# The output matrix of an attention layer: from seven block products (two by two by two) to fifteen (two by three by three)

## The chip, the cores and the metric

The kernel runs on one core of a Trainium2 chip. The metric is the device time of one execution in microseconds; the times shown are medians of several runs. The engines of a core are TensorE (PE in the profile, with PEld for its weight loads), VectorE (DVE), ScalarE (ACT), GpSimd (POOL) and SyncE (SP), which in this kernel issues all DMAs.

## The reference

Two graph layers act on `x` of 128 graphs x 64 nodes x 768 features, that is 8192 rows of 768, with an adjacency matrix for each graph. All arithmetic is float32.

```python
# layer 0: a graph attention with 12 heads of 64, a gate, residual, layer norm
x = _layernorm(x + _L0_gnn_ref(x, adj, W, b, w_src, w_dst, H_w, H_b))
# layer 1: masked attention with 6 heads of 128, residual, layer norm
q = heads(x @ Wq + bq); k = heads(x @ Wk + bk); v = heads(x @ Wv + bv)
scores = einsum('bhqd,bhkd->bhqk', q, k) / sqrt(128)
probs = softmax(scores + where(adj, 0, -9e15))
ctx = einsum('bhqk,bhkd->bhqd', probs, v)          # back to rows of 768
x = _layernorm(x + ctx @ Wf + bf)
```

The change concerns the last line alone: the product of the context (8192 x 768) with `Wf` (768 x 768), the bias and the rows `x` that are added, and the norm.

## The kernel before

Rows are worked in tiles of 128 (two graphs); four tiles make a quad, and there are 16 quads. Phase A computes layer 0 for all tiles, stores its rows (`x1_there`), and computes layer 1's values (`v_there`). Phase B, the second half of the time, does the rest of layer 1, a quad at a time, in three rounds `f` = 0, 1, 2 of two heads each: queries (7 products), keys (7 products), then the "slab" `slab(Q, f)`: scores, masked softmax, transposes by DMA, context.

All large matrix products are made by a scheme with fewer multiplications than the plain one. Both operands are cut in two by two blocks; sums of blocks are formed on each side, and 7 products of blocks instead of 8 give the result (the Winograd form of Strassen's scheme). `TURNS` lists the seven: name, PSUM tile (of three), block of the tokens, block of the weights. A product's reader is called when it is done; some results are sums of several products, gathered in PSUM (a product adds onto what its tile holds) or by DVE.

For the output (`output`, line 1026) a group is two tiles `ya`, `yb` of one quad: their context's four blocks are 128 tokens x 384 features, `Wf`'s are 384 x 384. A product is three matmuls of 128 x 128 stationary tokens against 384 columns of weights. Each quad has two groups, so there are 32 of 7 products. `operands` (line 1003) forms the four sums of context blocks on DVE; `rows_of` (line 1013) loads the rows of the first layer from DRAM by SP and adds the bias on POOL (line 1023); in the group ACT copies the first product (1042), DVE makes six adds from PSUM (1047 to 1066), and POOL three adds of rows (1036). `normed` (1071) takes mean and variance on DVE, the power on POOL (335), scales on ACT (1077) and stores by SP (1079).

The order of work is written by a host-side clock, `Beat`: each product is one beat; work is queued "so many beats from now", a reader 1.5 beats after its product was issued. A generator started with `beat.start` is taken up again after as many beats as it yields. Every engine runs its instructions in the order in which they were so issued, and semaphores are put where one engine needs another. So times in beats set orders, not durations.

In quad `q` the round loop (1088 to 1108) issues queries, then (rounds 1 and 2) starts the previous quad's `operands` and `rows_of`, then keys, then the slab, then the previous quad's output group: group 0 in round 1, group 1 in round 2. Products have 5 PSUM tiles in phase B, taken in turn as they come free. The matrix `Wf` is loaded at the start of phase B into the place of `Wv` (12 DMAs of `matrix`, line 243), its four block sums made by POOL, and `last_bias` adds `bv @ Wf` to the bias.

Of the kernel before, what the change touches and what calls it, by code (L numbers as in the profile page):

```python
# [31 lines left out]
ALU = mybir.AluOpType  # L35
# [4 lines left out]
P = 128  # L40
N = 64
D = 768
KC = D // P
KH = KC // 2
HALF = D // 2
H0, E0 = 12, 64
H1, E1 = 6, 128
BANK = 512
# [8 lines left out]
W11, W21, W22, T1, T2, T3, N4 = range(7)  # L57
# [13 lines left out]
    ("P4", 1, X22, N4),  # L71
)

# [50 lines left out]
class Beat:  # L127
# [23 lines left out]
        time = self.now + after + 0.7  # L151
        self.at(time, lambda: step(time), order)

    def product(self, emit, then):
        emit()
        self.at(self.now + 1.5, then)
        self.tick()

    def tick(self):
        while self.events and self.events[0][0] < self.now + 1:  # L160
            heapq.heappop(self.events)[-1]()
        self.now += 1

    def until(self, there):
        while not there():
# [8 lines left out]
def two_layers(  # L174
# [21 lines left out]
    nc = tc.nc  # L196
    n_tiles = x.shape[0] // P
    n_quads = n_tiles // 4
    n_pairs = n_tiles // 2
    beat = Beat()  # L200
# [5 lines left out]
    def sb(pool, shape, tag, name, bufs=None, dtype=F32):  # L206
        return pool.tile(shape, dtype, tag=tag, name=name, bufs=bufs)
# [8 lines left out]
    bv_sb = const.tile([P, KC], F32, name="bv_sb")  # L216
# [3 lines left out]

    places = [const.tile([P, 7, KH, HALF], F32, name=f"w_{i}") for i in range(3)]
    place = {"w0": 0, "h_w": 1, "wv": 2, "wq": 0, "wk": 1, "wf": 2}
# [20 lines left out]
    def matrix(w, name, engine, gap):  # L243

        t = places[place[name]]
        blocks = w.rearrange("(k c p) (m n) -> k m p c n", k=2, p=P, m=2)
        for at, k, m in ((W11, 0, 0), (T3, 0, 1), (W22, 1, 1), (W21, 1, 0)):
            for c in range(KH):
                nc.sync.dma_start(t[:, at, c], blocks[k, m][:, c])
                yield gap  # L250
        yield 3
        for to, a, b in ((T1, T3, W11), (T2, W22, T1), (T3, W22, T3), (N4, W21, T2)):
            for c in range(KH):
                engine.tensor_tensor(t[:, to, c], t[:, a, c], t[:, b, c], ALU.subtract)
                yield gap
        ready[f"{name}_sb"] = t
# [30 lines left out]
    def sums_of_tokens(engine, s, b11, b12, b21, b22):  # L287

        if engine is nc.vector:
            plus(s[:, 0], b21, b22)  # L290
            plus(s[:, 1], s[:, 0], b11, ALU.subtract)
            yield 1
            plus(s[:, 2], b11, b21, ALU.subtract)
            plus(s[:, 3], b12, s[:, 1], ALU.subtract)
        else:
            engine.tensor_tensor(s[:, 0], b21, b22, ALU.add)
            engine.tensor_tensor(s[:, 1], s[:, 0], b11, ALU.subtract)
            yield 1
            engine.tensor_tensor(s[:, 2], b11, b21, ALU.subtract)
            engine.tensor_tensor(s[:, 3], b12, s[:, 1], ALU.subtract)  # L300
# [47 lines left out]
    def in_zone(at, *shape):  # L348
        size = math.prod(shape)
        letters = " ".join("abc"[: len(shape)])  # L350
        sizes = dict(zip("abc", shape))
        return zone[:, at : at + size].rearrange(f"p ({letters}) -> p {letters}", **sizes)
# [507 lines left out]
    blocks = {}  # L860
# [9 lines left out]


    def phase_b(pb, ps_b):
        beat.start(matrix(wf, "wf", nc.gpsimd, 1), 2)
        bf_sb = row(bf, "bf_sb", pb)

        def last_bias():

            for m, parts in enumerate((((0, W11), (1, W21)), ((0, W11), (0, T1), (1, W22)))):
                ps = sb(dense[0], [P, BANK], "dense", f"bias_ps_{m}")[:, 0:HALF]
                steps = [(k * KH + c, wb, c) for k, wb in parts for c in range(KH)]  # L880
                for i, (at, wb, c) in enumerate(steps):
                    nc.tensor.matmul(  # L882
                        ps,
                        lhsT=bv_sb[:, at : at + 1].to_broadcast([P, P]),
                        rhs=ready["wf_sb"][:, wb, c, :],
                        start=(i == 0),
                        stop=(i == len(steps) - 1),
                    )
                to = bf_sb[:, m * HALF : (m + 1) * HALF]
                nc.vector.tensor_tensor(to, to, ps, ALU.add)  # L890

        def part(name):
            return sb(pb, [P, HALF], "part", name, 7)

        def load(Q):

# [106 lines left out]
        def operands(Q, i):  # L1003

            while not Q.get("done"):
                yield 1
            q, c = Q["q"], Q["c"][i]
            s = sb(pb, [P, 4, KH, P], "sc", f"sc_{q}_{i}", 1)
            b = [c[:, 0, :, 0], c[:, 1, :, 0], c[:, 0, :, 1], c[:, 1, :, 1]]
            yield from sums_of_tokens(nc.vector, s, *b)  # L1010
            Q["ob", i] = b + [s[:, k] for k in range(4)]

        def rows_of(Q, i):
            q = Q["q"]
            for k in range(2):
                t = 4 * q + 2 * k + i
                y = sb(pb, [P, D], "y", f"y_{t}", 4)
                nc.sync.dma_start(y, x1_there[t])
                Q["y", i, k] = y
            yield 2  # L1020
            for k in range(2):
                y = Q["y", i, k]
                nc.gpsimd.tensor_tensor(y, y, bf_sb, ALU.add)  # L1023
                yield 1

        def output(Q, i):
            q = Q["q"]
            ya, yb = Q["y", i, 0], Q["y", i, 1]
            lo, hi = slice(0, HALF), slice(HALF, D)
            u = {}  # L1030
            name = f"o_{q}_{i}_"

            def with_rows(k, of, y, m):
                def work():
                    u[k] = part(f"{name}{k}")
                    nc.gpsimd.tensor_tensor(u[k], u[of], y[:, m], ALU.add)  # L1036

                beat.soon(work)

            def p1(ps):  # L1040
                u[1] = part(f"{name}1")
                nc.scalar.copy(u[1], ps)
                with_rows(4, 1, yb, lo)

            def p6(ps):
                u[2] = part(f"{name}2")
                nc.vector.tensor_tensor(u[2], u[1], ps, ALU.add)
                with_rows(5, 2, ya, hi)

            def p2(ps):  # L1050
                nc.vector.tensor_tensor(ya[:, lo], ya[:, lo], ps, ALU.add)

            def p5(ps):
                u[3] = part(f"{name}3")
                nc.vector.tensor_tensor(u[3], u[1], ps, ALU.add)
                with_rows(6, 3, yb, hi)

            def p7(ps):
                nc.vector.tensor_tensor(yb[:, hi], u[6], ps, ALU.add)

            def p4(ps):
                nc.vector.tensor_tensor(yb[:, lo], u[4], ps, ALU.add)
                beat.start(normed(yb, 4 * q + 2 + i), 0)

            def p3(ps):
                nc.vector.tensor_tensor(ya[:, hi], u[5], ps, ALU.add)
                beat.start(normed(ya, 4 * q + i), 0)

            by_token(name, Q["ob", i], ready["wf_sb"], dict(P1=p1, P2=p2, P3=p3, P4=p4, P5=p5, P6=p6, P7=p7))

        def normed(y, t):
            scale = variance_to_scale(y, EPS, f"1_{t}")
            rs = next(scale)
            yield 1
            next(scale, None)
            yield 1
            nc.scalar.activation(y, y, AF.Identity, bias=rs[:, 1:2], scale=rs[:, 0:1])
            yield 1
            nc.sync.dma_start(out[t * P : (t + 1) * P, :], y)

        Q, before = quads[0], None

        def at_place(q, f):

            return (None, 0, 1)[f]

        load(Q)
        for q in range(n_quads + 1):
            for f in range(3):
                if q < n_quads and (q or f):  # L1090
                    queries(q, f, blocks, part)
                if q == 1 and f == 0:
                    last_bias()
                if before and at_place(q, f) is not None:
                    i = at_place(q, f)
                    beat.start(operands(before, i))
                    beat.start(rows_of(before, i))
                if q < n_quads:
                    then = None
                    if f == 2 and q + 1 < n_quads:  # L1100
                        then = lambda xb: blocks.update({xb: load_block(q + 1, xb)})
                    if q or f:
                        keys(q, f, blocks, part, then)
                    beat.start(slab(Q, f), 1)
                if before and at_place(q, f) is not None:
                    beat.until(lambda: ("ob", i) in before)
                    output(before, i)
            before, Q = Q, quads.get(q + 1)
# [57 lines left out]
```

## Time and profile before

| what | us |
|---|---|
| median of 3 runs | 2870.66 (2870.18 to 2870.84) |
| the profiled execution's own time | 2870.47 |
| its span, first to last instruction | 2868.7 |
| PE busy | 2819.2 |
| DVE busy | 1864.5 |
| ACT busy | 1324.9 |
| POOL busy | 1149.5 |

The profile is of one execution. Its parts used below: busy time per engine; the chain of work that ended last; groups of instructions by line, with operation, tiles, shapes, count, then busy time and mean duration, then the idle time of the engine before them and what ended it; and the timeline, which gives start, length, engine, line, operation and count. Durations of pipelined instructions overlap, so distances between starts are used for PE. An fp32 matmul shows as two MATMUL records.

### The profile page before, as it was taken

To read this page: it belongs to the slowest core of one execution; us is meant where nothing else is said; L and a number is where in the kernel's file an instruction comes from. 1 tells how busy PE (TensorE), PEld (TensorE's weight loads), DVE (VectorE), ACT (ScalarE), POOL (GpSimd) and SP (SyncE) were. 2 spreads that over 40 slices of the span, in tenths; PEclk is the share of its full clock that TensorE was granted. 3 is DMA by queue.
4 is the path that set the end of the run, shared out by engine and by line. 5 is a ranking of instruction groups with operands and counts; after the bars stand their busy time and mean duration, and the time that the engine had idled before them with its cause. 6 is when DMAs were issued, how large, how long until landed. Compare 5 with 4: busy or idle time off the path is not lost.

```text
span 2868.7 us, 42091 instructions
## 1 busy us (share of the span) xinstructions
PE 2819.2 (98%) x15586; PEld 1924.7 (67%) x15586; DVE 1864.5 (65%) x3567; ACT 1324.9 (46%) x1594; POOL 1149.5 (40%) x1022
## 2 busy tenths in 40 slices
PE   7899999999999999999899999999999999999998
PEld 4455555555555555555577878778787787877775
DVE  6888888888888888888634444444444444444444
ACT  2655665665665665655433333334333333333332
POOL 6656666665665665665412121221111211112113
PEclk9999999999999999999999999999999999999999
DMA  6666766666666766766655345534455443454432
GB/s 205 161 166 169 179 165 170 182 163 171 181 164 169 186 160 167 188 164 193 194 132 124 92 113 131 120 98 103 102 131 124 99 108 96 128 124 108 110 94 77
DMA packets 626285, 409.50 MB, mean 143 GB/s; under 512 B 440224, under 2 KB 572320, under 8 KB 626080
## 3 DMA queue, kind: packets, MB, share of 16 engines
q1 hardware_dynamic: 626080, 406.81, 55.0%
q8 instruction: 123, 2.02, 0.3%
q14 instruction: 82, 0.67, 0.1%
HBM read 186.69 MB, written 119.93 MB: 107 GB/s over the span
## 4 chain that ended last, share of the span: by engine, by line
PE 94%; DVE 2%; DMA 1%; ACT 0%; issue 0%; POOL 0%; SPq 0%; POOLq 0%; DVEq 0%; ACTq 0%
PE o L311 15%; PE k L407 15%; PE q L407 15%; PE v L311 15%; PE g L311 14%; PE h L311 14%; PE f_all L707 2%; PE s_ps L920 2%; PE c_ps L976 2%; DMA th_d<-bc_e 0%; PE bias_ps L882 0%; DVE th_d L651 0%; ACT bc_e L698 0%; DMA elu_turned<-xg_parts 0%; DVE st L328 0%
## 5 line engine op out<-in xcount | busy, mean ns | idle before, releaser
L311 PE MATMUL h<-w,zone 128*128 128x384 f32 x1320 | 445.8, 494 | 21.0 <-ACT h L498 12.2
L407 PE MATMUL q<-zone,w 128*128 128x256 f32 x2016 | 450.1, 381 | 3.5 <-issue 1.2
L407 PE MATMUL k<-zone,w 128*128 128x256 f32 x2016 | 446.2, 381 | 0.9 <-ACT k_u L387 0.9
L311 PE MATMUL g<-w,zone 128*128 128x384 f32 x1320 | 441.3, 489 | 4.6 <-DVE gate L552 3.8
L407 PEld LDWEIGHTS q<-zone,w 128*128 128x128 f32 x2016 | 381.3, 190 | 64.7 <-issue 3.4
L407 PEld LDWEIGHTS k<-zone,w 128*128 128x128 f32 x2016 | 380.6, 190 | 57.0 <-issue 5.0
L1023 POOL TENSOR_TENSOR y<-y,bf_sb 128x768 f32<-128x768 f32 x64 | 114.8, 1815 | 704.1 <-DMA y<-x_there 640.6
L311 PEld LDWEIGHTS h<-w,zone 128*128 128x128 f32 x1320 | 250.3, 192 | 193.4 <-ACT h L498 13.4
L311 PEld LDWEIGHTS g<-w,zone 128*128 128x128 f32 x1320 | 247.5, 190 | 176.6 <-DVE gate L552 13.3
L311 PE MATMUL o<-w,sc 128*128 128x384 f32 x768 | 268.0, 493 | 2.8 <-DVE sc L280 2.8
L311 PE MATMUL v<-w,x_sums 128*128 128x384 f32 x768 | 258.5, 486 | 1.8 <-DVE x_sums L280 1.8
L335 POOL TENSOR_TENSOR rs<-rs,power 128x1 f32<-128x1 f32 x128 | 71.2, 556 | 459.3 <-DVE rs L333 459.3
L627 POOL TENSOR_TENSOR bc_e<-th_d,w_dst_sb 128x768 f32<-128x768 f32 x64 | 119.9, 1874 | 290.4 <-ACT th_d L522 253.0
L311 PEld LDWEIGHTS v<-w,x_sums 128*128 128x128 f32 x768 | 145.7, 190 | 104.1 <-DVE x_sums L280 3.1
L311 PEld LDWEIGHTS o<-w,sc 128*128 128x128 f32 x768 | 144.1, 191 | 99.9 <-DVE sc L280 3.8
L311 PE MATMUL o<-w,cT 128*128 128x384 f32 x576 | 203.3, 489 | 0.5 <-ACT cT L986 0.5
L1036 POOL TENSOR_TENSOR o<-o,y 128x384 f32<-128x384 f32 x96 | 107.4, 1119 | 182.0 <-issue 82.0
L990 ACT COPY parts<-c_ps 128x1024 uint16<-128x1024 uint16 x94 | 95.4, 1015 | 149.8 <-PE c_ps L976 149.8
L311 PEld LDWEIGHTS o<-w,cT 128*128 128x128 f32 x576 | 108.0, 190 | 72.5 <-issue 2.6
L622 POOL TENSOR_SCALAR zone<-zone 128x768 f32<-128x768 f32 x64 | 137.2, 2144 | 0.0
L615 ACT ACTIVATE gate<-gate 128x768 f32<-128x768 f32 x64 | 53.9, 843 | 167.4 <-DVE gate L558 118.5
L698 ACT COPY bc_e<-th_d 128x1536 uint16<-128x1536 uint16 x64 | 123.3, 1927 | 14.6 <-DMA th_d<-bc_e 14.6
(161 smaller groups left out, 4492.6 us busy)
## 6 DMA issues: line engine op xcount, KB each, us to landing
zone<-ops_there SPq DMA_DIRECT2D x224, 192.0 KB, 4.7
zone<-in_xT SPq DMA_DIRECT2D x32, 768.0 KB, 6.6
zone<-in_x SPq DMA_DIRECT2D x64, 384.0 KB, 3.8
bc_e<-there SPq DMA_DIRECT2D x128, 192.0 KB, 3.5
x_there<-mix SPq DMA_DIRECT2D x64, 384.0 KB, 4.2
ops_there<-x_sums SPq DMA_DIRECT2D x32, 768.0 KB, 3.3
v_there<-v SPq DMA_DIRECT2D x128, 192.0 KB, 2.6
v<-v_there SPq DMA_DIRECT2D x128, 192.0 KB, 3.8
```

Source lines behind the costliest of these rows:

```text
L311: nc.tensor.matmul(ps, lhsT=blocks[xb][:, c, :], rhs=w[:, wb, c, :], start=(c == 0 and to not in begun), stop=(c == KH - 1), skip_group_ch ...
L335: nc.gpsimd.tensor_tensor(rs[:, 0:1], rs[:, 0:1], power, ALU.pow)
L407: nc.tensor.matmul(ps, lhsT=w[:, wb, c, f * P : (f + 1) * P], rhs=blocks[xb][:, c, :], start=(c == 0 and to not in begun), stop=(c == KH - 1),
L622: nc.gpsimd.tensor_scalar(xs, xs, 1.0, None, ALU.add)
L627: nc.gpsimd.tensor_tensor(bc, th, w_dst_sb, ALU.mult)
L698: nc.scalar.copy(halves(e), by_halves(d))
L707: nc.tensor.matmul(f_all[b * N : (b + 1) * N, at : at + E0 + 1], lhsT=e[rows, hd // 2 * P + b * N : hd // 2 * P + (b + 1) * N], rhs=(h[row ...
L920: nc.tensor.matmul(s_ps[b * N : (b + 1) * N, i, r, :], lhsT=qT[:, r, at], rhs=kT[:, r, at], start=True, stop=True,)
L976: nc.tensor.matmul(c_ps[cols, r, i, :], lhsT=sT[rows, i, cols], rhs=v_of, start=True, stop=True)
L990: nc.scalar.copy(by_halves(parts), halves(c_ps[:, r].rearrange("p i t -> p (i t)")))
L1023: nc.gpsimd.tensor_tensor(y, y, bf_sb, ALU.add)
L1036: nc.gpsimd.tensor_tensor(u[k], u[of], y[:, m], ALU.add)
```

## The change

The output's product is cut otherwise: the group's two tiles of tokens by three parts of the inner dimension by three parts of the columns. A context block is now 128 tokens x 256 features, a weight block 256 x 256, and the plain way would need 18 block products; a scheme with 15 is used. A product is two matmuls against 256 columns.

- `FIFTEEN` lists the products: PSUM tile (of six), block or sum of the context, block of the weights, and the places (of six: two tiles by three thirds) onto which the PSUM tile is added or from which it is subtracted. A PSUM tile gathers up to five products and is read after each of them.
- The reads go straight into the rows `y` on DVE, in place: 16 per group. The ACT copy, the six DVE adds and the three POOL adds are gone.
- `operands` makes eleven sums of 256 features x 128 tokens instead of four of 384, one per yield, and is started before the queries of its round rather than after. For the very last group most of these are made on POOL, in the zone that held the query operands.
- `rows_of` is started earlier: group 0's rows in round 2 of its own quad, group 1's in round 0 of the next, and it waits (in host order) until the bias is ready and the previous quad's rows of the same group have been sent out. The ring of row buffers still has four.
- `Wf` comes in nine DMAs of 256 KB, its blocks' sums are 15 POOL operations of 512 columns, and the bias is made in three parts between the first quad's queries.
- `Beat.product` and `tick` take a length; an output product counts 2/3 of a beat. The pool of parts has 5 buffers of 256 columns instead of 7 of 384.

```diff
+FIFTEEN = (
+    (0, "3", 9, ((-1, 1),)),
+    (2, "A2", 6, ((1, 0),)),
+    (1, "12", 0, ((-1, 3),)),
+    (0, "11", 7, ((1, 4),)),
...
+    (0, "1", 8, ((1, 0), (-1, 2))),
+    (5, "6", 13, ((-1, 4),)),
+    (1, "0", 10, ((1, 5),)),
+)
...
-    def product(self, emit, then):
+    def product(self, emit, then, length=1):
         emit()
-        self.at(self.now + 1.5, then)
-        self.tick()
+        self.at(self.now + 1.5 * length, then)
+        self.tick(length)
...
-        beat.start(matrix(wf, "wf", nc.gpsimd, 1), 2)
...
+        def last_matrix():
+            blocks = wf.rearrange("(c k p) (m n) -> k m p c n", k=3, p=P, m=3)
+            for k in range(3):
+                for m in range(3):
+                    nc.sync.dma_start(wf_sb[:, 3 * k + m], blocks[k, m])
+                    yield 1
+            yield 4
+            for m in range(3):
+                last_bias(m)
+                yield 1
+            ready["bias"] = bf_sb
+            for to, a, b, op in (
+                (9, 0, 7, ALU.add),
...
+            ):
+                nc.gpsimd.tensor_tensor(wf_sb[:, to], wf_sb[:, a], wf_sb[:, b], op)
+                yield 2
...
 # operands
-            s = sb(pb, [P, 4, KH, P], "sc", f"sc_{q}_{i}", 1)
-            b = [c[:, 0, :, 0], c[:, 1, :, 0], c[:, 0, :, 1], c[:, 1, :, 1]]
-            yield from sums_of_tokens(nc.vector, s, *b)
-            Q["ob", i] = b + [s[:, k] for k in range(4)]
+            A = [c[:, :, k, m] for m in range(2) for k in range(3)]
+            last = Q["q"] + 1 == n_quads and i == 1
+            s = in_zone(0, 11, 2, P) if last else sb(pb, [P, 11, 2, P], "sc", f"sc_{Q['q']}_{i}", 1)
+            of = Q["ob", i] = {f"A{k}": a for k, a in enumerate(A)}
+            sums = (
+                ("3", 1.0, "A0", "A2", ALU.subtract),
+                ("12", -1.0, "3", "A3", ALU.subtract),
...
+            for k, (name, sign, a, b, op) in enumerate(sums):
+                of[name] = s[:, k]
+                if last and sign == 1.0:
+                    nc.gpsimd.tensor_tensor(s[:, k], of[a], of[b], op)
+                else:
+                    nc.vector.scalar_tensor_tensor(s[:, k], of[a], sign, of[b], ALU.mult, op)
+                yield 1
...
 # rows_of
+            while "bias" not in ready or q and not all(quads[q - 1].get(("out", i, k)) for k in range(2)):
+                yield 1
...
 # output
+            for at, xb, wb, to in FIFTEEN:
+                beat.until(lambda: xb in of)
+                begun = at in sums
+                if not begun:
+                    sums[at] = sb(dense[0], [P, BANK], "dense", f"o_{q}_{i}_{at}")[:, 0:THIRD]
+                ps = sums[at]
+                def emit():
+                    for c in range(2):
+                        nc.tensor.matmul(ps, lhsT=of[xb][:, c, :], rhs=wf_sb[:, wb, c, :],
...
+                def read(ps=ps, to=to):
+                    for sign, b in to:
+                        k, n = divmod(b, 3)
+                        part_of = y[k][:, n * THIRD : (n + 1) * THIRD]
+                        nc.vector.tensor_tensor(part_of, part_of, ps, ALU.add if sign > 0 else ALU.subtract)
+                        left[k] -= 1
+                        if not left[k]:
+                            beat.start(normed(y[k], 4 * q + 2 * k + i), 0)
+                beat.product(emit, read, 2 / 3)
...
 # the round loop
+                if f == 2 and q < n_quads:
+                    beat.start(rows_of(Q, 0))
+                if f == 0 and before:
+                    beat.start(rows_of(before, 1))
+                if before and at_place(q, f) is not None and (q < n_quads or f == 1):
+                    beat.start(operands(before, at_place(q, f)))
+                    if q == n_quads and f == 1:
+                        beat.start(operands(before, 1), 5)
                 if q < n_quads and (q or f):
                     queries(q, f, blocks, part)
-                if q == 1 and f == 0:
-                    last_bias()
-                if before and at_place(q, f) is not None:
-                    i = at_place(q, f)
-                    beat.start(operands(before, i))
-                    beat.start(rows_of(before, i))
```

## The prediction

> **What bounds the kernel now.** I read the page first, to see which engine carries the time.
>
> ```profile
> span 2868.7 us, 42091 instructions
> PE 2819.2 (98%) x15586; PEld 1924.7 (67%) x15586; DVE 1864.5 (65%) x3567; ACT 1324.9 (46%) x1594; POOL 1149.5 (40%) x1022
> PE 94%; DVE 2%; DMA 1%; ACT 0%; issue 0%; POOL 0%; SPq 0%; POOLq 0%; DVEq 0%; ACTq 0%
> ```
>
> TensorE (PE) is busy 98% of the span and is 94% of the chain that ended last. The change lies in the second layer alone, so next I took the stretch of one quad there, engine by engine (the columns after the length are PE, PEld, DVE, ACT, POOL):
>
> ```profile
> 1618.80:1707.80 89.00, 89.00 (x532) 68.97 (x528) 40.04 (x89) 32.14 (x48) 16.89 (x18) 1.00 0.43 112
> ```
>
> 89.00 of 89.00 us are PE; DVE has 49 us free. So a quad is worth exactly what its matmuls take. Then the timeline of PE over one output group:
>
> ```profile
> 1653.09 2.10 PE L311 MATMUL o<-w,cT 128*128 128x384 f32 x6
> 1655.03 2.10 PE L311 MATMUL o<-w,sc 128*128 128x384 f32 x6
> 1657.06 1.15 PE L920 MATMUL s_ps<-zone 128*64 128x64 f32 x32
> 1658.14 2.20 PE L311 MATMUL o<-w,sc 128*128 128x384 f32 x6
> 1660.18 2.10 PE L311 MATMUL o<-w,cT 128*128 128x384 f32 x6
> 1662.11 4.03 PE L311 MATMUL o<-w,sc 128*128 128x384 f32 x12
> 1665.98 2.10 PE L311 MATMUL o<-w,cT 128*128 128x384 f32 x6
> 1667.92 0.38 PE L407 MATMUL q<-zone,w 128*128 128x256 f32 x1
> ```
>
> Starts count here, since durations overlap. 12 records of 384 columns take 1662.11 to 1665.98, 322.5 ns each. The next 42 records of 256 columns (q) run from 1667.92 to 1677.07, where the slab's c_ps begins: 217.9 ns, and k takes 218.0. A matmul is two records, so an output product of before is 6. Each entry into another stream costs about 0.1 us (2.03 for 1.94).
>
> What the other engines pay per operation:
>
> ```profile
> L383 DVE TENSOR_TENSOR k_u<-k_u,k 128x256 f32<-128x256 f32 x96 | 40.3, 421 | 118.1 <-ACT parts L990 68.8 <-PE k L407 45.9 <-ACT k_u L387 3.3
> L280 DVE SCALAR_TENSOR_TENSOR sc<-cT 128x384 f32<-128x384 f32 x64 | 36.4, 568 | 0.5 <-ACT cT L998 0.5
> L1023 POOL TENSOR_TENSOR y<-y,bf_sb 128x768 f32<-128x768 f32 x64 | 114.8, 1815 | 704.1 <-DMA y<-x_there 640.6
> ```
>
> [...] sums of L280 have a median of 549 ns and took 1.77 us once, while L1023 ran. A read of PSUM has one SBUF input and is free of it (L383: 410 to 423 ns throughout).
>
> **The change, part by part.**
>
> *Products.* A group (32 of them, two per quad) goes from 42 records of 384 to 15 products of 2 matmuls, 60 records of 256: 42 x 322.5 = 13.545 us, 60 x 218.0 = 13.08 us, so 0.465 us less. Slab interruptions are as many as before. For the 30 groups inside quads: **-13.95 us**.
>
> *Reads.* Out: an ACT copy (476 ns), six DVE adds (554) and three POOL adds of 384 (1119). In: 16 DVE adds of 256, taken as 421 ns like L383. Each product also gets a wait: its PSUM tile is kept over three products, so a product waits for the read of three before it. I laid one group out on DVE in program order, first product at 0, a product 0.87 us, the slab's scores from 2.71 to 3.79, a read 0.17 us after its product (L1047 after 1657.06), independent DVE operations 0.08 us closer than their durations (timeline). Scores add 3.91 to 4.60, maximum to 5.32, third read to 5.66, two reads and the subtraction between 5.8 and 7.16, reads 6 and 7 to 8.84, sum and reciprocal to 9.67, read 8 to 10.02, scaling to 10.62, read 9 to 10.96, read 11 to 12.33. The products that wait for reads 3, 8, 9 and 11 start at 6.51, 10.86, 11.74 and 13.48: the smallest margin is 0.78 us. The twelfth product's two reads and the first tile's statistics end near 15.1, so the last two reads come 0.7 us after the group, and the next queries' first use of DVE, at +2.8, is met or late by 1 us against the 2.1 us that its PSUM tile leaves. Cost on PE: 0, covered by these margins.
>
> *Sums of operands.* Four of 384 become eleven of 256. [...] 2.3 to 4.6 us a group. They are spread over queries' and keys' products, where DVE was idle between reads (0.8 to 2.2 us each). With the reads DVE gains 2 x 5.7 = 11.4 us per quad, 40 to 51 of 88: it isn't a bound. Cost 0; [...] the two rows' adds of a quad half fall at places where at most two sums follow, ahead of reads with 2.1 us of room.
>
> *Rows a third of a quad ahead.* The same four loads and four L1023 per quad. But a second load's y buffer is now one whose store was just issued: SP waits for that store to land, and behind it in SP stands the transpose of the second half of the slab's context (L991), then on ACT its two copies (L998), then the keys' activation L390, and for that PE's next scores. SP around it, before:
>
> ```profile
> 1677.58 5.59 SPq L909 DMA_DIRECT2D v<-v_there  x8
> 1683.26 1.27 SPq L991 DMA_TRANSPOSE s<-parts  x1
> 1684.63 1.60 SPq L991 DMA_TRANSPOSE sT<-parts  x1
> ```
>
> From the first queries of a quad: v loads until 11.4, store issued by 11.8, transpose to 13.1, first row load to 13.5, store landed 14.1 to 14.8 (2.3 us and more), second transpose issued near 14.8, landed 5.0 later (the one instance behind two row loads, at 2804.8) near 19.8; copies 1.4 and activation 0.5 end near 21.7; scores are due at 22.1. Bounds: 0, or about 1 us per quad if the store lands 1.4 us later. I take 0.1 us for 15 quads, **+1.5 us**.
>
> *Weights and bias.* 30 records of 384 (9.68 us, 1489.3 to 1499.0) become 36 of 256 in three pieces, 7.85 + 3 x 0.1: **-1.5 us**. Nine loads in place of twelve; by the SP spacing of 0.7 us from 1444.3, with the transpose between, they land by 1459.5, and the first bias product stands at 1460.8. POOL's 15 sums of 512 columns (996 ns for 384, so 1.33 us each), spaced two products apart, end near 1502; the first output is at 1529. If the cover is gone, up to 3 us once.
>
> *The end.* The last two groups take 32.96 us from 2828.33, 27.1 of them matmuls. Waits and half clock make the rest:
>
> ```profile
> 2830.35 0.91 PE L311 MATMUL o<-w,cT 128*128 128x384 f32 x2 [0.46 <-ACT cT L986]
> 2834.03 4.22 PE L311 MATMUL o<-w,sc 128*128 128x384 f32 x7 [2.76 <-DVE sc L280]
> ```
>
> Records after 2834.03 start 0.64 us apart until 2837.4 [...]. After: 26.2 us of matmuls; the first product now needs a sum, so 1.9 us pass (copies 0.56 and 0.69, sum 0.42, waits), then 1.3 us before the second and third sums; with half a slow stretch (1.7 us) and one lock, 31.4: -1.6. The transposed weights' copy (0.68 us idle at 2825.7) is covered by output products, -0.7; the last read stands behind the other tile's statistics, +0.6. **-1.7 us**, with -5 and +3 as ends.
>
> Sum: -13.95 + 1.5 - 1.5 - 1.7 = -15.7 us. Against the profiled execution's 2870.47 us: 2854.8; the median of before is 0.2 above that execution, so 2855.0.
>
> **Rivals.**
> 1. *DVE falls behind in the output slot* and products wait. For: 16 reads, the slab's chain and the statistics fill some 12 of 14.3 us in order, and any DVE wait (for ACT's exponential, say) holds all reads behind it. Against: margins of 0.78 us. One product's time lost per group is 32 x 0.87 = 28 us: 2883. It decides from 15.7 / 30 = 0.52 us per group on: beyond that the kernel is slower than before.
> 2. *The SP chain is late* by 0.5 to 1.1 us per quad: +6 to +15, 2861 to 2870. For: transposes behind row loads took 5.0 us against a median of 4.0. Against: it only shows past 22.1 us.
> 3. *The products don't do what they say*: two matmuls and a wait per product cost 225 ns a record instead of 218; 1920 x 7 ns = 13.4, 2868. For: never seen with this stationary side. Against: q and k have a wait per product and run at 218.0.
>
> **Numbers.** Forecast 0.61 (own range 2849 to 2860), rival 1 0.14, rival 2 0.15, rival 3 0.07, other 0.03. 0.2% (5.7 us) is about what a measurement of this kernel can tell from no change. Faster: the forecast and most of rival 2, 0.75; same: rival 3 and the tail of 2, 0.11; slower 0.14. The range runs from all gains in full with the better end (2849) to rival 2 and 3 (2868).
>
> **What would show it.** PE should start an output product every 0.87 us and a quad should take 88.1 us. Idle PE at output products released by DVE's reads means rival 1; at the scores, released by ACT L390 or its like, rival 2; records more than 218 ns apart without a releaser, rival 3. DVE should read near 51 us a quad. Wrong sizes are likeliest in the end and in the second transpose's landing.

## The result, and the profile after

The changed kernel takes 2868.27 us (median of 20 runs, 2863.83 to 2874.32) against 2870.89 us for the kernel before on the same chip (20 runs, 2869.08 to 2874.94). The ratio is 0.999, with a 95% interval of 0.9983 to 0.9996. So 2.6 us were gained where 15.7 were forecast. That is under the 0.2% (5.7 us) that the prediction called no change, though the interval does not reach 1, and it lies 0.3 us outside the predicted range.

From the page of the changed kernel: its span (2866.4 us; the execution's own time is 2868.3), the busy times, the shares of the chain that ended last, and the output's products and reads.

```profile
span 2866.4 us, 43840 instructions
PE 2804.1 (98%) x16168; PEld 2038.1 (71%) x16168; DVE 2039.1 (71%) x4103; ACT 1305.3 (46%) x1562; POOL 1067.2 (37%) x938
PE 89%; DMA 4%; DVE 2%; SPq 1%; ACT 1%; issue 1%; POOL 0%; POOLq 0%; ACTq 0%; DVEq 0%
L1135 PE MATMUL o<-w,sc 128*128 128x256 f32 x1364 | 326.7, 384 | 4.7 <-DVE sc L1102 4.7
L1148 DVE TENSOR_TENSOR y<-y,o 128x256 f32<-128x256 f32 x512 | 206.7, 415 | 126.7 <-PE o L1135 120.1
```

PE lost 15.1 us of busy time, about the gain that was worked out. But its share of the chain fell from 94% to 89%, and DMA's rose from 1% to 4%: that chain now runs through transfers more often.

Two stretches, engine by engine (columns as before: length, then PE, PEld, DVE, ACT, POOL). The first is one whole quad. The second is of the same length, cut from a quad whose first queries start at 1951.12 us and which took 89.13 us:

```profile
1598.30:1686.37 88.07, 88.05 (x566) 75.80 (x564) 51.52 (x123) 30.04 (x45) 11.41 (x13) 1.00 0.48 112
1951.25:2039.30 88.05, 86.81 (x561) 74.86 (x560) 50.79 (x123) 30.59 (x46) 10.22 (x12) 1.00 0.46 110
```

In the first PE is busy throughout and the quad takes the 88.1 us of the prediction. In the second 1.24 us of PE are missing. The next quad is worse (91.8 us); here is PE at its first scores:

```profile
2040.25 2.75 PE L442 MATMUL q<-zone,w 128*128 128x256 f32 x12
2045.22 1.15 PE L991 MATMUL s_ps<-zone 128*64 128x64 f32 x32 [2.22 <-ACT zone L425]
2046.31 8.43 PE L442 MATMUL q<-zone,w 128*128 128x256 f32 x30
```

The scores were due 2.68 us after 2040.25 and began 2.29 us late, released by ACT's activation of the keys (L425). ACT ahead of that:

```profile
2032.68 0.37 ACT L422 COPY k_u<-k 128x256 f32<-128x256 f32 x1 [3.42 <-PE k L442]
2038.21 1.39 ACT L1069 COPY cT<-s 128x512 uint16<-128x512 uint16 x2 [5.15 <-DMA s<-parts]
2043.46 1.38 ACT L1069 COPY cT<-sT 128x512 uint16<-128x512 uint16 x2 [3.86 <-DMA sT<-parts]
2044.71 0.46 ACT L425 ACTIVATE zone<-k,bk_sb 128x256 f32<-128x256 f32 x1
```

ACT sits idle 5.15 and 3.86 us in front of the copies of the context (L1069), whose transposes have not landed, with the activation behind them. And SP, which issues the transposes (L1062):

```profile
2026.68 5.53 SPq L980 DMA_DIRECT2D v<-v_there  x8
2032.30 0.55 SPq L1163 DMA_DIRECT2D out<-y  x1
2032.94 1.71 SPq L1062 DMA_TRANSPOSE s<-parts  x1
2034.70 2.96 SPq L1113 DMA_DIRECT2D y<-x_there  x2
2037.76 1.25 SPq L1062 DMA_TRANSPOSE sT<-parts  x1
```

Between the two transposes stand the two row loads; the second waits 1.5 us for the store of L1163 to land. The second transpose is issued at 2037.76 us and lands 5.6 us later, and its copy on ACT starts at 2043.46.

Where the time went, from the PE timelines of the two profiled executions (a difference below zero is a gain):

| stretch | forecast | changed kernel | row loads behind the transposes |
|---|---|---|---|
| span's start to the queries ahead of layer 1's first scores | 0 | +2.6 | -0.8 |
| to the first output product | -1.5 | -1.6 | -2.2 |
| to the start of the 30th group, the last that lies in a quad | -12.0 | -4.4 | -16.1 |
| to the span's end | -2.2 | +1.1 | +2.0 |
| sum | -15.7 | -2.3 | -17.1 |

The forecast's third row is 29 groups at -0.465 and the transposes' +1.5; its fourth is -0.465 and the end's -1.7. The first stretch has the same instructions on every engine in both kernels, so its +2.6 is no effect of the change: over the executions shown here, that point came between 1435.6 and 1439.7 us. The last column is an experiment below. The scores of the first third waited 10.1 us over 14 quads (the 12 query records ahead of them and the wait took 47.6 us in place of 37.5): 0.5 us in the first four quads, 9.5 in the other ten.

### The profile page after: what moved, and what is told of

Same layout as the page of the kernel before. It is cut to its first block, busy times and chain, and to the rows that moved or that the text cites. A ratio compares the mean times of both kernels' runs of the same rounds, so it can differ in the third digit from the quotient of the medians.

```text
span 2866.4 us, 43840 instructions
## 1 busy us (share of the span) xinstructions
PE 2804.1 (98%) x16168; PEld 2038.1 (71%) x16168; DVE 2039.1 (71%) x4103; ACT 1305.3 (46%) x1562; POOL 1067.2 (37%) x938
## 4 chain that ended last, share of the span: by engine, by line
PE 89%; DMA 4%; DVE 2%; SPq 1%; ACT 1%; issue 1%; POOL 0%; POOLq 0%; ACTq 0%; DVEq 0%
PE v L346 15%; PE o L1135 15%; PE h L346 14%; PE g L346 14%; PE q L442 14%; PE k L442 12%; PE f_all L742 2%; PE s_ps L991 2%; PE c_ps L1047 2%; DMA out<-y 2%; DMA sT<-parts 2%; SPq L980 1%; ACT cT L1069 0%; PE bias_ps L951 0%; DMA s<-parts 0%
## 5 line engine op out<-in xcount | busy, mean ns | idle before, releaser
L346 PE MATMUL h<-w,zone 128*128 128x384 f32 x1320 | 446.2, 494 | 21.7 <-ACT h L533 12.5
L442 PE MATMUL q<-zone,w 128*128 128x256 f32 x2016 | 461.6, 384 | 3.8 <-issue 1.2
L1135 PE MATMUL o<-w,sc 128*128 128x256 f32 x1364 | 326.7, 384 | 4.7 <-DVE sc L1102 4.7
L1148 DVE TENSOR_TENSOR y<-y,o 128x256 f32<-128x256 f32 x512 | 206.7, 415 | 126.7 <-PE o L1135 120.1
L1135 PEld LDWEIGHTS o<-w,sc 128*128 128x128 f32 x1364 | 256.1, 191 | 43.8 <-DVE sc L1102 6.0
L1118 POOL TENSOR_TENSOR y<-y,bf_sb 128x768 f32<-128x768 f32 x64 | 118.4, 1865 | 342.4 <-DMA y<-x_there 313.9
L1161 ACT ACTIVATE y<-y,rs 128x768 f32<-128x768 f32 x64 | 65.7, 1026 | 157.8 <-POOL rs L371 157.8
L1009 ACT ACTIVATE s<-s 128x512 f32<-128x512 f32 x48 | 30.1, 626 | 226.2 <-DVE s L1007 226.2
L1102 DVE SCALAR_TENSOR_TENSOR sc<-cT 128x256 f32<-128x256 f32 x217 | 113.9, 525 | 22.9 <-ACT cT L1069 22.8
```

Source lines behind the costliest of these rows:

```text
L346: nc.tensor.matmul(ps, lhsT=blocks[xb][:, c, :], rhs=w[:, wb, c, :], start=(c == 0 and to not in begun), stop=(c == KH - 1), skip_group_ch ...
L442: nc.tensor.matmul(ps, lhsT=w[:, wb, c, f * P : (f + 1) * P], rhs=blocks[xb][:, c, :], start=(c == 0 and to not in begun), stop=(c == KH - 1),
L1102: nc.vector.scalar_tensor_tensor(s[:, k], of[a], sign, of[b], ALU.mult, op)
L1135: nc.tensor.matmul(ps, lhsT=of[xb][:, c, :], rhs=wf_sb[:, wb, c, :], start=(c == 0 and not begun), stop=(c == 1), skip_group_check=True,)
L1148: nc.vector.tensor_tensor(part_of, part_of, ps, ALU.add if sign > 0 else ALU.subtract)
```

## The experiments

The theory after the result: the second transpose is issued behind the row loads in SP's queue, and its copies stand ahead of the keys' activation in ACT's. Rivals: the rows' bytes slow the transpose by sharing the DMA engines, wherever they stand in a queue; or the products do not bring what they should. Unless another base is named, each run is the changed kernel with the one edit shown. Each ratio is to the runs of the kernel before that were made beside it on the same chip (their medians lie between 2870.19 and 2871.94 us).

**Row loads behind the transposes** (SP's order alone).

```diff
-                    beat.start(rows_of(before, 1))
+                    beat.start(rows_of(before, 1), 6.5)
```

> The changed kernel with the second group's rows started 6.5 beats later, so that on SP their two loads stand behind both transposes of the context instead of ahead of the second. ACT's order is the same. Queue theory: the second transpose lands some 3 us earlier, waits at the scores under 1 us in all, 2858 us; POOL's adds of the rows then fall later, on the first sums of the next round, which may cost up to 2 us. Bandwidth theory: the transposes still land late behind the value loads, waits at the scores stay above 6 us, 2864 to 2868. Gain-isn't-there theory: 2866 or more.

2854.57 us; ratio 0.9949 (0.9936 to 0.9963). PE waits at no scores of the first third. SP and then ACT at the same place of the same quad:

```profile
2027.00 1.98 SPq L1062 DMA_TRANSPOSE s<-parts  x1
2029.07 1.87 SPq L1062 DMA_TRANSPOSE sT<-parts  x1
2030.99 1.05 SPq L1113 DMA_DIRECT2D y<-x_there  x2
```

```profile
2033.39 1.38 ACT L1069 COPY cT<-sT 128x512 uint16<-128x512 uint16 x2
2034.63 0.47 ACT L425 ACTIVATE zone<-k,bk_sb 128x256 f32<-128x256 f32 x1
```

ACT still has the copies first, but they no longer wait for the second transpose. The row loads take 1.05 us to issue and not 2.96, since by then the store has landed, 4.7 us from its issue: the second load waited 0.03 us for it.

Two things bring the second transpose forward. Over the ten quads that had waited in the changed kernel, it was issued 4.4 us behind the first transpose there and 1.7 here, and it took 4.7 us to land there and 4.0 here (medians over each transfer's issue and landing in the two traces). So 2.7 of 3.4 us are SP's order; the other 0.7 the sharing rival may claim, since the rows' bytes moved behind the transposes as well.

**Keys' activation first** (ACT's order alone; the copies of the third round start two beats later).

```diff
-                yield 3
+                yield 5 if f == 2 else 3
```

> The changed kernel with one order changed on ACT: in round 2's slab the four context copies are issued two beats later, so that the keys' activation (L425) of the next quad's round 0 stands ahead of them and no longer waits for the transpose by DMA. SP's order is the same. Queue theory (the 10.1 us that PE waited at the scores in the changed kernel come from this activation standing on ACT behind copies whose transpose SP issued late): those waits go to under 1 us in all, 2858 us, 0.45% faster than before. Gain-isn't-there theory (products of 256 columns lose it elsewhere, or the wait only moves on to DVE's sums or the next products): 2866 or more, with PE idle at output products or queries. Bandwidth theory (DMA is saturated there): as the queue theory, since PE no longer depends on it.

2855.57 us; ratio 0.9949 (0.9936 to 0.9961). ACT, same place:

```profile
2032.01 0.47 ACT L425 ACTIVATE zone<-k,bk_sb 128x256 f32<-128x256 f32 x1 [3.51 <-PE k L442]
2038.95 1.40 ACT L1069 COPY cT<-sT 128x512 uint16<-128x512 uint16 x2 [4.07 <-DMA sT<-parts]
```

The second transpose lands as late as in the changed kernel (3.2 us after the first queries of the quad start, 3.1 there), ACT sits idle 4.07 us in front of its copy, and it does no harm: the scores wait nowhere. So the loss needs both orders together.

**Seven beats a group**: the fifteen products count seven beats of the clock as the seven products did, not ten.

```diff
-                beat.product(emit, read, 2 / 3)
+                beat.product(emit, read, 7 / 15)
```

> The changed kernel with an output product counted as 7/15 of a beat in place of 2/3, so that a group is 7 beats as before the change and the slab's later steps stand where they stood among the queries' and keys' products (keys' activation ahead of the context copies, stores and row loads ahead of the value loads). Queue theory: the waits at the scores go, 2858 us; at most 2 us is lost where the context is done a beat later than the sums want it. Gain-isn't-there theory: 2866 or more. Bandwidth theory: 2858 as well, since the activation no longer waits.

2857.48 us; ratio 0.9957 (0.9944 to 0.9969), no waits at these scores. SP and then ACT at the same place:

```profile
2021.53 2.47 SPq L1113 DMA_DIRECT2D y<-x_there  x2
2024.05 0.43 SPq L970 DMA_DIRECT2D a8b<-in_adj  x1
2025.35 5.51 SPq L980 DMA_DIRECT2D v<-v_there  x8
2030.96 1.28 SPq L1062 DMA_TRANSPOSE s<-parts  x1
2032.34 1.72 SPq L1062 DMA_TRANSPOSE sT<-parts  x1
```

```profile
2031.36 0.47 ACT L425 ACTIVATE zone<-k,bk_sb 128x256 f32<-128x256 f32 x1 [2.60 <-PE k L442]
2035.15 1.39 ACT L1069 COPY cT<-s 128x512 uint16<-128x512 uint16 x2 [3.32 <-DMA s<-parts]
```

The keys' activation is ahead of the copies, the row loads are ahead of the value loads, and the two transposes stand together. The clock's length of a group is therefore what set both orders: with ten beats instead of seven, the slab's later steps fall three products earlier among the next queries and keys. From the first output product to the 30th group this run takes 1263.39 us, 1.0 less than with the loads behind; its end is 3.0 longer.

**Rows ahead alone**: the kernel before, with only the loads moved (and the flags that they wait for).

```diff
+                if f == 2 and q < n_quads:
+                    beat.start(rows_of(Q, 0))
+                if f == 0 and before:
+                    beat.start(rows_of(before, 1))
...
-                    beat.start(rows_of(before, i))
```

> The kernel before with one part of the change alone: the token rows are loaded a third of a quad ahead (first group's at the head of the last third, second group's at the head of the next first third), with seven products and the old operands. Theory (the loads only hurt together with the new order on ScalarE): before, the keys' activation stands ahead of the context copies on ScalarE, so a transpose that lands a few us later holds nothing up; 2868 to 2872 us, no wait of TensorE at the first scores. Rival (the loads ahead of the transposes hurt by themselves): the scores of the first third wait 0.4 to 2 us a quad as in the changed kernel, 2876 to 2890 us.

2868.47 us (13 runs); ratio 0.999 (0.9982 to 0.9998). From the first output product to the last group in a quad it takes 1280.46 us, as the kernel before does to a hundredth. ACT there:

```profile
2042.65 0.47 ACT L390 ACTIVATE zone<-k,bk_sb 128x256 f32<-128x256 f32 x1 [2.60 <-PE k L407]
2047.32 1.39 ACT L998 COPY cT<-s 128x512 uint16<-128x512 uint16 x2 [4.20 <-DMA s<-parts]
2048.58 1.38 ACT L998 COPY cT<-sT 128x512 uint16<-128x512 uint16 x2
```

The copies end 3.7 us after the next queries start (2046.3), too late for the scores 2.7 us after that start, but the activation was done before the copies began. Loading rows ahead is harmless by itself. (SP has the loads ahead of the value loads here. The changed kernel's SP order together with this ACT order is the run with the keys' activation first.)

**Rows from another queue**: GpSimd issues the row loads at the same beats.

```diff
-                nc.sync.dma_start(y, x1_there[t])
+                nc.gpsimd.dma_start(y, x1_there[t])
```

> The changed kernel, its token rows loaded from GpSimd's queue in place of SyncE's, at the same beats. If the place in SyncE's queue decides (the second transpose is issued behind two row loads), the transpose is issued about 3 us earlier, lands at 2.9 to 4 us from its issue, and TensorE does not wait at the first scores: 2853 to 2858 us. If the DMA engines that they share decide (the rows' 786 KB move in front of the transpose whatever the queue), the transpose still lands late and the waits of 0.4 to 2.3 us a quad stay: 2862 to 2868 us.

2865.56 us (16 runs, 2859.8 to 2870.16); ratio 0.998 (0.9973 to 0.9988). Neither expectation holds as written. In the profiled execution the scores' waits fell from 10.1 us to 2.2, and the stretch from the first output to the last group in a quad from 1276.10 to 1268.94 us; 4.5 us over the 1264.40 of the run with the loads behind are left, 2.4 of them at queries. At the end the two last groups take 35.55 us, 2.4 more than in the changed kernel. GpSimd now waits for the store:

```profile
2037.54 0.54 POOL L1113 DMA_DIRECT2D y<-x_there  x1 [10.54 <-DMA out<-y]
2038.09 1.84 POOL L1118 TENSOR_TENSOR y<-y,bf_sb 128x768 f32<-128x768 f32 x1
```

The wait that SP had for the store is now GpSimd's, whose queue has less behind it that PE waits for. That speaks for SP's place, but it is no clean test of the sharing rival: in the quad shown the second row load goes out only at 2037.54 us, behind both transposes. And the transposes do land later in this run. The second took 4.1 to 8.4 us from its issue over the 14 quads (median 5.6; 3.6 to 5.7, median 3.9, with the loads behind), and the three scores that still waited are those of the three quads where it took over 7 us. What made it late there was not separated. The profiled execution (2862.42 us) is one of the shorter ones, and what makes these runs spread over 10 us was not followed up.

**Stores first.** In the four quads from 1598 to 1951 us both stores of a group stand ahead of the value loads and the row loads ahead of both transposes (0.5 us of waits in all four together); in the other ten the second store comes behind the value loads, and the row loads between the transposes (9.5 us). Two steps of the clock fall on the same beat there. This edit sets the stores a tenth of a beat earlier.

```diff
-                            beat.start(normed(y[k], 4 * q + 2 * k + i), 0)
+                            beat.start(normed(y[k], 4 * q + 2 * k + i), -0.1)
```

> The changed kernel with the norm started a tenth of a beat earlier, which decides the tie between a store and the value loads the same way in all quads: both stores stand on SP ahead of the value loads, and the row loads ahead of both transposes (the order of the first output quads, which waited 0.54 us at the scores in all four, against 9.5 us in the other ten). Queue theory: waits at the scores 0 to 0.2 us a quad, 2858 to 2861. Bandwidth theory: it doesn't matter who is first, 2864 to 2868. Gain-isn't-there theory: 2866 or more.

2883.44 us (2876.26 to 2885.73); ratio 1.004 (1.0027 to 1.0052): slower, against all that was expected. The scores' waits did go, to 0.6 us, but a new wait came. First its line in the waits, then DVE in the quad at 1770:

```profile
PE q L442 <- DVE zone L428: 15.1, 5, 4.4
```

```profile
1773.70 1.83 DVE L972 TENSOR_SCALAR biasb<-a8b 128x256 f32<-128x256 uint8 x1 [6.80 <-DMA a8b<-in_adj]
1775.45 0.47 DVE L428 SCALAR_TENSOR_TENSOR zone<-q,bq_sb,q_u 128x256 f32<-128x256 f32 x1
1775.85 0.47 DVE L434 SCALAR_TENSOR_TENSOR zone<-q,bq_sb,q_u 128x256 f32<-128x256 f32 x1
```

Here the next quad's adjacency (L970) is issued behind two stores and two row loads. DVE waits 6.80 us to convert it, and the reads of the queries' products (L428, L434) stand behind the conversion, so PE waits for them. DVE waited 56.8 us there in 14 quads, against 20.5 in the changed kernel. The 30 stretches of 18 query records between a context and the keys took 140.0 us, not 119.6. All but 1.0 us of the difference comes from the four quads in which the two row loads stand ahead of the adjacency; in the other ten only the two stores do, and DVE's wait of 2.8 to 4.6 us reached PE once.

Three runs on this base test that reading. The first loads and converts the adjacency in the second third of the quad:

```diff
+            if f == 1 and q + 1 < n_quads:
+                adjacency(quads[q + 1])
```

> Stores first (as in the run that was slower), and the next quad's adjacency is loaded and turned into a bias a third earlier, so that no store or row load stands before it on SyncE. Theory (that run's new wait is VectorE held at the adjacency's conversion, 56.8 us in 14 quads against 20.5, with the queries' reads queued behind it): the queries behind the contexts take 3.99 us in every quad (119.6 us for 30 pieces, not 140), 2850 to 2857 us. Rival (the queries wait for something else that the stores hold up, such as the value loads or transposes): 2872 to 2885 us, the same long pieces.

2898.35 us; ratio 1.01 (1.0084 to 1.0115). The place was badly chosen: there the first group's stores stand ahead, in five quads with two row loads. DVE waited 66.6 us for the load, the queries took 152.1 us. The wait moved with the load, which speaks for the reading, but it mended nothing. So next the load alone was put into the first third, the conversion left at its place:

```diff
+            if f == 0 and q + 1 < n_quads:
+                adjacency(quads[q + 1])
```

> Stores first, with only the load of the next quad's adjacency moved: it is issued in the first third of the quad, where no store of two groups stands just ahead of it (in the run before, it had been put in the second third, behind the first group's stores, with its conversion; that only moved the wait to another third, VectorE held 66.6 us at the conversion). The conversion stays at its place. Theory (VectorE held at the conversion, the queries' reads queued behind it, is all of what stores first cost): VectorE's wait there goes from 56.8 us to under 5, the queries behind the contexts take 3.99 us in every quad (119.6 us for the 30 pieces), 2852 to 2858 us. Rival (something else that stands behind the stores, the value loads or the transposes, is as late): 2865 us or more, the long pieces stay.

2855.41 us; ratio 0.9943 (0.993 to 0.9955). DVE never waits for the adjacency, and the queries are back at 119.6 us. This run also bears on the sharing rival: the row loads go out ahead of both transposes in all 14 quads, so their bytes are in front of the second transpose, which took 5.3 us to land (median, against 3.9 with the loads behind). The scores waited only 0.7 us in all. So the transpose landed later with those bytes in front of it, but the orders of SP and ACT decided whether PE felt it.

The last leaves the load and converts on GpSimd:

```diff
-            nc.vector.tensor_scalar(bias, a8, 1.0, -NEG, ALU.subtract, ALU.mult)
+            nc.gpsimd.tensor_scalar(bias, a8, 1.0, -NEG, ALU.subtract, ALU.mult)
```

> Stores first, the adjacency loaded where it was, its conversion on GpSimd in place of VectorE. Same theory: VectorE has nothing in its row that waits for the load, so the queries' reads go on: no long pieces behind the contexts, 2852 to 2862 us, with up to 5 us lost where the bias or the rows behind it on GpSimd are late in turn. Rival (the queries wait for another load): 2870 to 2883 us.

2858.41 us; ratio 0.9952 (0.994 to 0.9965). GpSimd waits 73.1 us for the same load, and the queries take 119.6 us all the same. So the late load cost the queries only through the engine on which their reads stood behind it. It is not free on GpSimd: in the profiled execution (2861.68 us, the longest of the five) the scores of the first third waited 5.5 us in six quads, and why was not followed up.

**The end.** On the base with the row loads behind, the last group's additions to its rows come four beats later and its sums three beats later.

```diff
-            yield 2
+            yield 6 if q + 1 == n_quads and i == 1 else 2
...
-                        beat.start(operands(before, 1), 5)
+                        beat.start(operands(before, 1), 8)
```

> Rows behind the transposes (the kernel that took 2854.6 us), and at the end the last group's additions of the bias to its rows four beats later and its sums three beats later, so that GpSimd's additions do not run while VectorE makes the sums that the group before it waits for. Theory (VectorE's sums are held while GpSimd works on the rows: one sum took 2.02 us in place of 0.41, and TensorE waited 2.2 us for the next): the last two groups take 31.5 to 32.5 us, not 34.1, 2852 to 2853.5 us. Rival (the granted clock at the end, 0.67 to 0.86 there, sets it): 2854 to 2855 us.

2853.09 us; ratio 0.9939 (0.9927 to 0.9952), 1.5 us less than its base, with intervals that overlap. In the traces the two last groups take 30.72 us, not 34.09. DVE without the edit and with it:

```profile
2819.86 2.02 DVE L1102 SCALAR_TENSOR_TENSOR zone<-zone,cT 128x256 f32<-128x256 f32 x1
```

```profile
2826.60 0.42 DVE L1102 SCALAR_TENSOR_TENSOR zone<-zone,cT 128x256 f32<-128x256 f32 x1
```

Without it, this sum runs beside POOL's addition of a row (L1118, 2819.62 to 2821.60) and PE then waits 2.20 us for the sum behind it; with it that wait is gone. The clock is the rival: without the edit, eight PE records behind that wait took 3.0 us in place of 1.7 (granted clock 0.86 and 0.80 from 2820 to 2830 us); with it, records are slow only at the group's start, as they are in both (four take 1.6 to 1.9 us there, in place of 0.87). So of the 3.4 us 1.6 are waits of PE, which the edit took away, and the rest are slow records, which need not be the edit's doing: the two runs with the adjacency loaded earlier have the same waits at the end, the longest 1.82 us, and the eight records behind that one took 1.83 us in the first and 3.23 in the second. What starts a slow stretch stays open.

**All three edits together**: loads behind, activation first, the end.

> The changed kernel with the three edits that helped, together: the row loads behind the transposes, the keys' activation ahead of the copies, the end's additions later. Theory: each of the first two alone already takes away all waits at the scores, so together they give no more than one of them, and the end keeps its 1.5 us: 2852 to 2854 us. Rival (each still leaves a part of the loss): 2845 to 2850 us.

2851.64 us (2851.33 to 2853.34); ratio 0.993 (0.9917 to 0.9944), the lowest median of the runs, though its interval overlaps those of the runs with one or two of the edits. The stretch from the first output to the last group in a quad is 1264.40 us, within 0.01 us what the loads behind give alone: the two orders guard against the same loss, and either edit takes all of it.

## Why the prediction was wrong

- **What bounds the kernel: right.** PE's own work set the time of every quad that nothing disturbed (88.05 of 88.07 us busy in the first stretch shown).
- **Products: right, and undersized.** A record of 256 columns takes 218.0 ns and a product starts every 0.87 us. The gain is 0.60 us a group, not 0.465: before, a group took 13.80 us in its quad, not the 13.545 of its records alone, and after it takes 13.20, not 13.08. What lies over the records' own time was put in neither sum, and it shrank from 0.25 to 0.12 us. Over 29 groups that is 17.25 us. In the run with the loads behind 16.1 are left, because five early contexts, which now stand among the queries, took 1.2 to 1.3 us in place of 1.03; with seven beats, where the contexts stand between queries and keys as before, 17.1 are left. So it is luck that the quad shown took the 88.07 us of the forecast: two groups gained 1.19 us and one context lost 0.26. An undisturbed late quad takes 87.82.
- **Reads and rival 1: right.** DVE reads about 51 us a quad, as worked out, and PE waits for no read of an output product inside a quad. The layout of a group on DVE held: counted from the group's first product, and from read 0, read 9 was to end at 10.96 us and ended at 10.96, read 11 at 12.33 and 12.37 (the group at 1707.44). None of the 512 reads took over 423 ns; the three that ran beside a row's addition on POOL (L1118) took 406 to 422. That eleven sums of operands take 4.6 us a group was the author's estimate, 0.42 us for one (median 417 ns where no row's addition ran beside it, up to 2.05 us where one did). PE waited for sums in the last two groups alone (4.7 us).
- **Rows a third of a quad ahead: the step that failed.** "I take 0.1 us for 15 quads, +1.5 us" measured +11.7: 1276.10 less the 1264.40 that the same kernel takes with SP's order mended. Of these, 10.1 stood at the scores; the other 1.7 came in the queries right behind the longest of the waits (2.29 us), which took 8.26 us in place of 6.58 at a granted clock of 0.79. The chain was the right one, named from SP to PE's scores, and it is rival 2 that happened, at a chance of 0.15. The forecast of that rival, 2861 to 2870 us, holds the result. The chain's times were too short at each link. From the quad's first queries (2020.9 in the quad shown, the worst of 14), with the forecast first: first transpose issued until 13.1, 13.8; store landed 14.8, some 16.4 (5.0 us from its issue, not 2.3 to 3); second transpose issued 14.8, 16.9; landed 19.8, 22.5; activation's end 21.7, 24.3. Due was 22.1. A margin of 0.4 us at the end of five links was costed at almost nothing, and "about 1 us per quad if the store lands 1.4 us later" was written down as a bound but given little weight: it landed 1.6 later, and the scores' waits came to 0.7 us a quad on average.
- **What the step had not seen** is that the place of the keys' activation behind the copies is itself a result of the change. Before, ACT has it ahead of them, as this quad of the kernel before shows:

```profile
1683.59 0.47 ACT L390 ACTIVATE zone<-k,bk_sb 128x256 f32<-128x256 f32 x1 [2.60 <-PE k L407]
1687.39 1.39 ACT L998 COPY cT<-s 128x512 uint16<-128x512 uint16 x2 [3.32 <-DMA s<-parts]
```

The prediction took the new order for granted and priced only SP's part, so it did not ask what a beat more or less would do.
- **Bias: right** (-1.5 forecast, -1.6 measured to the first output product).
- **The end: wrong sign.** -2.2 forecast with the 30th group's gain, +1.1 measured. Up to the last context it went as forecast (-1.3, forecast -1.2), and so did what follows the last product (+0.4, forecast +0.6). From the last context to the last product +2.0 came in place of -1.6. In the forecast's 31.4 us for it the matmuls, the two waits and half a slow stretch make 31.1 (before, records started 0.64 us apart from 2834.03 to 2837.40 us, at a granted clock of 0.51), which leaves 0.3 for its "one lock", a sum held while a row's addition runs on POOL (before, one took 1.77 us). Measured, three sums were held (1.76, 0.94 and 0.96 us) and PE waited 0.90, 2.10 and 0.57 us behind the first product; the slow records (2825.49 to 2830.97 us, granted clock 0.50) cost 2.7 us, not 1.7:

```profile
2831.88 1.13 PE L1135 MATMUL o<-w,sc 128*128 128x256 f32 x4 [0.90 <-DVE sc L1102]
2839.43 2.00 PE L1135 MATMUL o<-w,sc 128*128 128x256 f32 x8 [2.10 <-DVE sc L1102]
```

For the kernel with the loads behind the forecast came near, 2855.0 against 2854.57 us, but that is luck in part. Against the forecast, its trace has 2.6 us more gain in the 29 groups and 4.2 less at the end, no price for the rows (1.5 forecast), 0.7 more gain around the bias, and 0.8 from the first stretch, which is chance.

## What to carry to other kernels

Where a host-side clock writes the order, a new length for one piece of work moves every step queued behind it on every engine: compare the two kernels' instruction order engine by engine, in an early quad and in a late one, before costing anything. A load into a buffer whose store was just issued held its whole queue here until that store landed (2.96 us for two loads, 1.05 without the wait), so put such a load behind everything that PE will soon wait for, or give it a queue where nothing urgent stands behind it. If a chain of several transfers is to end 0.4 us before it is due, as here, price it as late too, and see what two reordered instructions at its end would cost.

## What the runs showed of the hardware

- A store of 384 KB issued just behind eight value loads landed 5.0 us later, where the four stores from 1990 to 2080 us have a median of 2.7 us: a median from issue to landing says little where much stands ahead.
- In the quad shown the first DMA transpose landed 5.2 us from its issue, behind value loads and a store, and the second 5.6 us, behind row loads too; over the whole execution the medians are 3.2 (`s<-parts`) and 4.5 us (`sT<-parts`). The first transpose of that quad was slow whatever stood behind it: 5.2 us where row loads followed it, 5.1 where they stood behind both transposes, 5.4 where they came ahead of the value loads (rows alone), and 5.8 where one was issued from GpSimd's queue among the value loads.
- The queries ahead of layer 1's first scores started between 1435.6 and 1439.7 us in executions of kernels with the same instructions up to there: 4 us of spread that no single profile of this kernel can tell from an effect.
- A DVE sum of two SBUF tiles took 2.02 us beside a GpSimd addition of a row and 0.42 us without. In the changed kernel 39 of the 343 sums (L1102) ran over 0.1 us beside such an addition: 29 of them took over 1 us, the longest 2.05. None of the other 304 took over 0.97 us (median 0.417).
